# Attention and a ternary feed-forward net on one core: more blocks of P on their way, the looks at the weights in another order and without ScalarE, the flag made last

## The chip, the cores and the metric

The kernel runs on one core of a Trainium2 chip. The core has a matrix engine (TensorE, PE in the profile; its weight loads are PEld), three engines for elementwise work (VectorE or DVE, ScalarE or ACT, GpSimd or POOL) and SyncE (SP), which here only issues DMAs. The metric is device time in microseconds for one execution. Three runs of the kernel before gave 871.02, 871.73 and 874.87 us, median 871.73.

## The reference

```python
x: (2, 2048, 256)                                  # layer norm without weights, then
xn = layernorm(x)
q, k, v = xn @ Wq, xn @ Wk, xn @ Wv                # 256 x 256 each
attn = softmax(causal(q @ k.T) * 256 ** -0.5)
a = (attn @ v) @ Wo
h = silu(xn @ w1.T * s1) * (xn @ w2.T * s2)        # 1024 hidden, weights are -1, 0 or 1
h = gelu(h @ h1.T * s_h1); h = gelu(h @ h2.T * s_h2)
out = x + a + h @ w3.T * s3
```

All arrays are float32. The feed-forward weights are drawn from -1, 0 and 1, but the kernel may not take that for granted: it looks at them while it runs.

## The kernel before, in words

The program has two stages. The first is attention with everything beside it, to about 283 us in the profiled execution; the second is the feed-forward net, from there to the end. A flag, one number in memory, decides between two forms of the second stage: a fast one for weights that are whole and small (`ffn_ternary`), and a general one. All engines read the flag (L1175) and branch (L1176).

**Tiles.** The 2 x 2048 rows are eight blocks of 512 (n = 0 to 7, four to a batch), each of four tiles of 128 rows (t = 0 to 3). For one tile the keys come in blocks m of 512, up to n. `score(n, t, m)` is six products of 512 columns (L401: numbers are split in a high and a low part) into one of four PSUM banks; DVE copies the bank out and takes the row maximum (L410); after the last block ACT takes the exponentials (L422).

**Turning P.** The product of P with the values (`weigh`, L479 and L484: four products with 512 columns and four with 256 for a full block) needs P transposed. Small pieces are transposed by PE (L465). Most go another way, "by blocks": DVE transposes 32 x 32 squares (`turn_blocks`, L292), SP stores the result in DRAM (L297, d<-b), and SP fetches it back in another order, four DMAs to a unit of up to eight key tiles (`fetch_blocks`, L304, e<-d). Then `turn(n, t, m)` makes one block pT of it: ACT rounds the high part (L460), POOL subtracts for the low part (L461). There are two buffers for fetched units (pool `bp`, tile e) and four for pT (pool `ptp`, LEAD + 2 with LEAD = 2). `fetch_units` (L439) fetches the unit that is needed and, when a unit's first block is turned, one more.

**Order of work.** A planner written out by hand goes through the 32 tiles (loop at L721). In step j it scores tile j and weighs the tiles that are due: a tile by blocks is due 42000 columns of matrix work after its scores (DELAY_BLOCKS), others 9000. `weigh_steps` puts the turning of a block at most LEAD = 2 blocks ahead of the weighing (L518). `merged` interleaves both lists by their cost in columns. This gives the order in which the program is written; a scheduler with a model of the engines then fixes the order on each engine, and may move an instruction ahead of one that it holds to be waiting.

**The looks.** Beside this, `beside` (L642) spends every few thousand columns on one step of a list of looks at the weights, which are loaded by ACT's DMA queue into two buffers (stg, 128 x 1024). `low` is for w1, w2 and w3: POOL rounds w1 and w2 into their place for the second stage (L134, via L555), DVE masks the low bits (L558), ACT sums them (L560). `odd` is for h1 and h2: ACT takes absolute values (L565), DVE counts what is neither 0 nor 1 (L567); there are 16 such looks. For h1, DVE also forms four sums for the second stage (`sum_up`, L153), which SP stores. The order of the list is w1, w2, then in turns h1, h2 and w3 (L607 to L617). All these are put behind a marked instruction of the planner's on their engine (`tc.issue_after`). When no look is left, the flag is made: a maximum on DVE, a product of one number on PE (L744), a copy to memory on DVE (L745).

At the end PE makes the last quarter of a first product of the feed-forward net (L748 to L750, with L172), which is before the branch in PE's program.

**Second stage.** `ffn_ternary` multiplies by the seven-product scheme of Strassen and Winograd (L850); its first products are those of L172 with w1 and w2.

Of the kernel before, what the change touches and what calls it, by code (L numbers as in the profile page):

```python
# [9 lines left out]
F32 = mybir.dt.float32  # L10
F32R = mybir.dt.float32r
# [9 lines left out]
P = 128  # L21
TB = 512
# [10 lines left out]
LOOKS_FROM = 3  # L33
LEAD = 2
WARM = 14

# [3 lines left out]

SLOTS = {"h1": range(7), "h2": (0, 4, 1, 3, 2, 5, 6)}
LOW_BITS = 0xFFF

# [21 lines left out]
def attn_ffn_kernel(  # L65
# [123 lines left out]
    with ExitStack() as actx:  # L189
# [6 lines left out]
        sp = actx.enter_context(tc.tile_pool(name="sp", bufs=3))  # L196
        bp = actx.enter_context(tc.tile_pool(name="bp", bufs=2))
        ptp = actx.enter_context(tc.tile_pool(name="ptp", bufs=LEAD + 2))
        small = actx.enter_context(tc.tile_pool(name="small", bufs=4))
# [3 lines left out]
        xs, rstds, ks, qs, vs = {}, {}, {}, {}, {}  # L203
        turns = {"ps": 0, "b": 0, "q": 0}

# [4 lines left out]
        def bank():  # L210
            return in_turn("ps", ps_tiles)

        def load_x(n):
# [224 lines left out]

        def fetch_units(until, more):  # L439
            while units and (more or until not in fetched):  # L440
                more = more and until not in fetched
                n, t, u, k, d = units.pop(0)
                e = bp.tile([P, UK * P], F32, tag="e", name=f"e_{n}_{t}_{u}")[:, : k * P]
                fetched[n, t, u] = fetch_blocks(d, k, e)

        def turn(n, t, m):

            first = n - n % NB
            tiles = NT if m < n else t + 1
            w = tiles * P  # L450
            pT = ptp.tile([P, 2, TB], F32R, tag="pT", name=f"pT_{n}_{t}_{m}")
            state[n, t][m] = pT
            if by_blocks(n, t, m):
                u, at = divmod((m - first) * NT, UK)
                fetch_units((n, t, u * UK), at == 0)
                src = fetched[n, t, u * UK][:, ds(at, tiles)]
                hi, lo = (
                    pT[:, a, :w].rearrange("p (k i q) -> p k i q", k=tiles, q=Q) for a in range(2)
                )
                nc.scalar.copy(hi, src)  # L460
                nc.gpsimd.tensor_tensor(lo, src, hi.bitcast(F32), ALU.subtract)  # L461
                return
            pt = ps_t.tile([P, TB], F32, tag="pt", name=f"pt_{n}_{t}_{m}")
            for j in range(tiles):
                nc.tensor.transpose(  # L465
                    pt[:, ts(j, P)], state[n, t]["s"][:, ds((m - first) * TB + j * P, P)], ident
                )
            hi_lo(pT[:, 0, :w], pT[:, 1, :w], pt[:, :w])

        def weigh(n, t, m):  # L470
            first = n - n % NB
            st = state[n, t]
# [41 lines left out]
        def weigh_steps(g, until):  # L514

            steps = []
            while g < len(blocks) and blocks[g][0] <= until:
                while turned[0] <= min(g + LEAD, len(blocks) - 1) and (  # L518
                    turned[0] <= g or blocks[turned[0]][0] <= until + 1
                ):  # L520
                    b = blocks[turned[0]]
                    steps.append((0 if by_blocks(*b[1:]) else 2 * TB, lambda b=b: turn(*b[1:])))
                    turned[0] += 1
                _, n, t, m = blocks[g]
                steps.append((6 * TB if m < n else 6 * P * (t + 1), lambda b=blocks[g]: weigh(*b[1:])))
                g += 1
            return g, steps
# [34 lines left out]
        def odd(t):  # L562

            with tc.issue_after(marks["ACT"]):
                nc.scalar.activation(t, t, AF.Abs)  # L565
            with tc.issue_after(marks["DVE"]):
                nc.vector.scalar_tensor_tensor(  # L567
                    t, t, 0.0, t, ALU.not_equal, ALU.not_equal, accum_out=seen()
                )
# [36 lines left out]

        for src, dst in ((w1, w1_sb), (w2, w2_sb)):  # L607
            for c in range(src.shape[1]):
                item_low(src[:, c, :], dst[:, c, :])
        w3_at = list(range(0, HC, SC // D))  # L610
        for c in range(HK):
            item_factors(h1, factors["h1"], c)
            for k in (2 * c, 2 * c + 1):
                item_signs(h2[:, k, :])
# [104 lines left out]
        j = -1  # L719
        checked = False  # L720
        while until < len(tiles) - 1:  # L721
# [16 lines left out]
            merged(a, b, beside)  # L738
            if not looks and not checked:
                checked = True  # L740
                most = small.tile([P, 1], F32, tag="most", name="most")
                nc.vector.reduce_max(most, low_bits[:, : looked[0]], axis=AX.X)
                pf = bank()
                nc.tensor.matmul(out=pf[:1, :1], lhsT=most, rhs=ones, start=True, stop=True)  # L744
                nc.vector.tensor_copy(flag, pf[:1, :1])  # L745

        assert checked
        last_quarter = [bank(), bank()]  # L748
# [473 lines left out]
```

## Time and profile before

| | us |
|---|---|
| median of three runs | 871.73 |
| the profiled execution, its own time | 872.82 |
| its span, first to last instruction | 871.1 |
| PE busy in the span | 852.2 |
| DVE, ACT, POOL busy | 620.4, 504.9, 296.4 |
| start of the first L479, of the last quarter's L172, of the first L850 | 53.7, 283.6, 307.3 |

The profile is of one execution, taken by the hardware profiler. A row of the timeline has the start, the time that it covers, the engine, the line of the program, the operation, what it writes and reads, and in brackets the idle time ahead of it and who ended that. The windows give, for a stretch, the busy time of each engine and the share of full speed that was granted to PE's clock (PEclk). The end of a matrix product is modelled, and products overlap; the pace of PE is read from one start to the next.

### The profile page before, as it was taken

How to read it: one execution, taken by the hardware profiler on the slowest of the kernel's cores; microseconds unless marked ns; L12 is line 12 of the kernel's file. 1: busy time of each engine (PE TensorE's matmuls, PEld its weight loads, DVE VectorE, ACT ScalarE, POOL GpSimd, SP SyncE). 2: the span in 40 equal slices, each digit the busy share in tenths (PEclk: the TensorE clock that was granted, in tenths of full speed). 3: DMA queues.
4: the chain of work that ended last, by engine and by line, in shares of the span. 5: the costliest groups of instructions: out<-in, count | busy, mean ns of one | idle time of the engine just before them, and what ended most of it. 6: DMA issues, size and time to landing. Idle time of an engine off the chain costs nothing.

```text
span 871.1 us, 12205 instructions
## 1 busy us (share of the span) xinstructions
PE 852.2 (98%) x4280; PEld 720.1 (83%) x4280; DVE 620.4 (71%) x1065; ACT 504.9 (58%) x881; POOL 296.4 (34%) x242
## 2 busy tenths in 40 slices
PE   8999799999999999999999999999999999999997
PEld 5988688888887878888988888988888898888887
DVE  5687664784764699996596596569468648848764
ACT  2556556764666456677256586536557635657670
POOL 4034857433544476550142050025024003502300
PEclk8999989999999999999999999999999999999999
DMA  9876499766792898854334434432444431144411
GB/s 307 331 250 212 152 348 292 265 214 194 251 343 62 340 400 309 312 192 146 111 109 150 144 144 146 148 121 103 146 145 145 146 136 58 50 144 145 145 49 53
DMA packets 62679, 162.53 MB, mean 187 GB/s; under 512 B 6544, under 2 KB 36368, under 8 KB 53264
## 3 DMA queue, kind: packets, MB, share of 16 engines
q1 hardware_dynamic: 56048, 141.73, 46.6%
q10 hardware_dynamic: 5472, 15.73, 5.3%
q0 software_dynamic: 1088, 4.19, 1.2%
q8 instruction: 36, 0.59, 0.3%
q14 instruction: 35, 0.29, 0.1%
HBM read 120.21 MB, written 47.71 MB: 193 GB/s over the span
## 4 chain that ended last, share of the span: by engine, by line
PE 75%; DMA 9%; DVE 6%; issue 3%; ACT 3%; POOL 2%; SPq 2%; ACTq 0%; POOLq 0%; DVEq 0%
PE ps_own L850 23%; PE ps L850 23%; PE ps L172 5%; PE ps_own L172 5%; PE ps L401 5%; DMA e<-d 4%; PE ps_own L1011 4%; PE ps L1011 4%; POOL pT L461 2%; DMA d<-b 2%; PE ps L373 2%; PE po L479 2%; PE ps L357 2%; SPq L304 1%; DMA d_x<-b 1%
## 5 line engine op out<-in xcount | busy, mean ns | idle before, releaser
L401 PE MATMUL ps<-k,q 128*128 128x512 f32 (+3 forms) x480 | 109.6, 366 | 0.0
L461 POOL TENSOR_TENSOR pT<-e,pT 128x512 fp32r<-128x512 f32 (+3 forms) x60 | 74.8, 1264 | 72.5 <-ACT pT L460 55.6
L401 PEld LDWEIGHTS ps<-k,q 128*128 128x128 f32 x480 | 82.0, 189 | 12.2
L479 PE MATMUL po<-v,pT 128*128 128x512 f32 x272 | 79.6, 406 | 6.6 <-ACT pT L460 6.5
L982 POOL TENSOR_TENSOR rt<-rt,xt 128x1024 f32<-128x1024 f32 x8 | 21.5, 2706 | 165.2 <-issue 114.7
L871 ACT ACTIVATE k_h_u<-k_h_u,h_s_sb 128x512 f32<-128x512 f32 x64 | 45.9, 722 | 38.1 <-DVE k_h_u L870 37.5
L830 POOL TENSOR_TENSOR k_h_u<-k_h_p,k_h_u 128x512 f32<-128x512 f32 x16 | 23.2, 1452 | 123.1 <-ACT q L185 106.3
L479 PEld LDWEIGHTS po<-v,pT 128*128 128x128 f32 x272 | 48.1, 193 | 14.5 <-ACT pT L460 7.2
L410 DVE TENSOR_SCALAR_CACHE_REDUCE s<-ps 128x512 f32<-128x512 f32 (+3 forms) x80 | 47.1, 600 | 12.1 <-PE ps L407 8.1
L422 ACT ACTIVATE s<-s,low 128x1024 f32<-128x1024 f32 (+7 forms) x48 | 43.0, 898 | 21.7 <-DVE low L416 21.7
L292 DVE STREAM_TRANSPOSE b<-s 128x1024 f32<-128x1024 f32 (+3 forms) x30 | 33.5, 1128 | 22.8 <-ACT s L422 20.5
L460 ACT CAST pT<-e 128x512 fp32r<-128x512 f32 (+3 forms) x60 | 32.4, 574 | 27.4 <-DMA e<-d 25.0
L484 PEld LDWEIGHTS po<-v,pT 128*128 128x128 f32 x272 | 42.0, 190 | 6.5 <-POOL pT L461 1.7
L484 PE MATMUL po<-v,pT 128*128 128x256 f32 x272 | 46.9, 286 | 0.2 <-POOL pT L461 0.2
L186 DVE TENSOR_TENSOR q<-k_h_u,q 128x512 fp32r<-128x512 f32 x32 | 45.9, 1462 | 0.0
L889 POOL TENSOR_TENSOR k_h_p<-f_h_B,k_h_p 128x512 f32<-128x512 f32 x16 | 34.4, 2175 | 21.2 <-DVE h_h_T L186 21.2
L500 POOL TENSOR_TENSOR r<-r 128x256 f32<-128x256 f32 x32 | 24.4, 765 | 49.7 <-ACT r L499 49.7
L830 POOL TENSOR_TENSOR f_w_B<-f_w_B,f_w_B 128x512 f32<-128x512 f32 x16 | 26.0, 1646 | 33.0 <-DVE f_w_B L181 33.0
L172 PE MATMUL ps<-xh,w_sb 128*128 128x512 f32 x144 | 35.9, 392 | 0.0
L870 DVE TENSOR_TENSOR k_h_u<-ps_own,k_h_u 128x512 f32<-128x512 f32 x32 | 21.7, 686 | 17.8 <-PE ps_own L850 17.8
L871 ACT ACTIVATE k_h_p<-k_h_p,h_s_sb 128x512 f32<-128x512 f32 x32 | 22.8, 722 | 18.6 <-DVE k_h_p L870 18.6
L850 PE MATMUL ps<-q,w_h_A 128*128 128x512 f32 x128 | 31.2, 393 | 1.5 <-DVE f_w_B L181 1.5
(176 smaller groups left out, 2201.3 us busy)
## 6 DMA issues: line engine op xcount, KB each, us to landing
w_h_S<-factors_h SPq DMA_DIRECT2D x32, 1024.0 KB, 4.7
w_h_A<-factors_h SPq DMA_DIRECT2D x24, 1024.0 KB, 4.7
d<-b SPq DMA_DIRECT2D x18, 512.0 KB, 3.5
e<-d SPq DMA_DIRECT2D x72, 128.0 KB, 3.6
xT_d<-k SPq DMA_DIRECT2D x8, 1024.0 KB, 7.3
stg<-in_ffn_h_w ACTq DMA_DIRECT2D x16, 512.0 KB, 5.6
x<-in_attn_x SPq DMA_DIRECT2D x16, 256.0 KB, 5.9
factors_h<-xh SPq DMA_DIRECT2D x4, 1024.0 KB, 4.8
```

The costliest lines, as they stand in the source:

```text
L172: nc.tensor.matmul(out=p, lhsT=w[:, c, ts(o, P)], rhs=xh[:, c, a, :], start=(c == 0 and a == 0), stop=(c == DC - 1 and a == 1),)
L186: nc.vector.tensor_tensor(r[:, 1, :], f, r[:, 0, :].bitcast(F32), ALU.subtract)
L401: nc.tensor.matmul(out=ps[:, :w], lhsT=qs[n][:, c, a, ts(t, P)], rhs=ks[m][:, c, b, :w], start=(k == 0), stop=(m < n and k == 3 * DC - 1),)
L410: marks["DVE"] = nc.vector.tensor_scalar(st["s"][:, ds(at, w)], ps[:, :w], 1.0, None, ALU.mult, ALU.max, accum_out=st["tops"][:, m - first ...
L422: marks["ACT"] = nc.scalar.activation(st["s"][:, at], st["s"][:, at], AF.Exp, bias=low, accum_out=st["sums"][:, u // UK : u // UK + 1],).ins
L461: nc.gpsimd.tensor_tensor(lo, src, hi.bitcast(F32), ALU.subtract)
L479: nc.tensor.matmul(out=st["po"], lhsT=pT[:, 0, ts(j, P)], rhs=vs[m][:, j, :, :], start=(m == first and j == 0), stop=False,)
L484: marks["PE"] = nc.tensor.matmul(out=st["po"][:, 0, :], lhsT=pT[:, 1, ts(j, P)], rhs=vs[m][:, j, 0, :], start=False, stop=(m == n and j == ...
L830: nc.gpsimd.tensor_tensor(B["B12"][i], B["B22"][i], B["B12"][i], ALU.subtract)
L850: nc.tensor.matmul(out=out[o], lhsT=w[:, c, ts(o, P)], rhs=sets[right][c][:, a, :], start=(start and c == 0 and a == 0), stop=(c == HK - 1 ...
L871: nc.scalar.activation(C[k][o], r[o] if r else banks[o], AF.Gelu, scale=s[:, at : at + 1])
L1011: nc.tensor.matmul(out=ys[t][:, :D], lhsT=h[c][:, a, ts(t, P)], rhs=w3_sb[:, c, :], start=(c == 0 and a == 0), stop=(c == HC - 1 and a == 1),)
```

## The change

It does seven things.

1. Fetched units rotate over four memories instead of two, and blocks pT over six instead of four. The new memory is that of w1 (two more for units) and w2 (two more for blocks), which hold nothing until the looks at w1 and w2 put it there. From tile (6, 0) on (`WIDE`), units go to the four buffers of x and the blocks use the two own unit buffers in place of w2's.
2. `fetch_units` fetches whenever fewer than four units are fetched and not yet turned to the end.
3. A block that is turned by blocks may be turned four blocks ahead of the weighing (LEAD_BLOCKS = 4); one that PE transposes stays at two.
4. The looks at w1 and w2 move from the head of the list to behind h1's last item.
5. `odd` takes the absolute value on DVE, by masking the sign bit, and not on ACT.
6. The flag is made just ahead of the last weighing, its product behind the marked product on PE.
7. The pool `bp` goes.

```diff
+LEAD_BLOCKS = 4
+MAGNITUDE = 0x7FFFFFFF
-        bp = actx.enter_context(tc.tile_pool(name="bp", bufs=2))
-        ptp = actx.enter_context(tc.tile_pool(name="ptp", bufs=LEAD + 2))
+        ptp = actx.enter_context(tc.tile_pool(name="ptp", bufs=1))
...
+        pT_tiles = [ptp.tile([P, 2, TB], F32R, name=f"pT_{i}") for i in range(4)]
+        e_tiles = [ptp.tile([P, UK * P], F32R, name=f"e_{i}") for i in range(2)]
+        w_memory = [
+            [w.rearrange("p c h -> p (c h)")[:, ts(i, UK * P)] for i in range(2)] for w in (w1_sb, w2_sb)
+        ]
+        WIDE = (N - 2, 0)
+        def pT_tile(n, t):
+            more = e_tiles if (n, t) >= WIDE else w_memory[1]
+            tile = in_turn("pT", pT_tiles + more)
+            return tile if len(tile.shape) == 3 else tile.rearrange("p (a t) -> p a t", a=2)
+        def e_tile(n, t):
+            if (n, t) >= WIDE:
+                return xp.tile([P, NT, D], F32, tag="x", name=f"e_{n}_{t}").rearrange("p t d -> p (t d)")
+            return in_turn("e", e_tiles + w_memory[0]).bitcast(F32)
...
-        def fetch_units(until, more):
-            while units and (more or until not in fetched):
-                more = more and until not in fetched
+        def fetch_units():
+            while units and len(fetched) < 4:
                 n, t, u, k, d = units.pop(0)
-                e = bp.tile([P, UK * P], F32, tag="e", name=f"e_{n}_{t}_{u}")[:, : k * P]
-                fetched[n, t, u] = fetch_blocks(d, k, e)
+                fetched[n, t, u] = fetch_blocks(d, k, e_tile(n, t)[:, : k * P])
...
                 src = fetched[n, t, u * UK][:, ds(at, tiles)]
+                if at + tiles == fetched[n, t, u * UK].shape[1]:
+                    del fetched[n, t, u * UK]
...
+        def judge():
+            most = small.tile([P, 1], F32, tag="most", name="most")
+            nc.vector.reduce_max(most, low_bits[:, : looked[0]], axis=AX.X)
+            with tc.issue_after(marks["PE"]):
+                pf = bank()
+                nc.tensor.matmul(out=pf[:1, :1], lhsT=most, rhs=ones, start=True, stop=True)
+            nc.vector.tensor_copy(flag, pf[:1, :1])
         def weigh(n, t, m):
+            if (n, t, m) == (N - 1, NT - 1, N - 1):
+                judge()
...
-                while turned[0] <= min(g + LEAD, len(blocks) - 1) and (
-                    turned[0] <= g or blocks[turned[0]][0] <= until + 1
-                ):
+                while turned[0] < len(blocks):
                     b = blocks[turned[0]]
+                    lead = LEAD_BLOCKS if by_blocks(*b[1:]) else LEAD
+                    if turned[0] > g and (turned[0] > g + lead or b[0] > until + 1):
+                        break
...
         def odd(t):
-            with tc.issue_after(marks["ACT"]):
-                nc.scalar.activation(t, t, AF.Abs)
             with tc.issue_after(marks["DVE"]):
+                nc.vector.tensor_scalar(t.bitcast(U32), t.bitcast(U32), MAGNITUDE, None, ALU.bitwise_and)
                 nc.vector.scalar_tensor_tensor(
                     t, t, 0.0, t, ALU.not_equal, ALU.not_equal, accum_out=seen()
                 )
...
-        for src, dst in ((w1, w1_sb), (w2, w2_sb)):
-            for c in range(src.shape[1]):
-                item_low(src[:, c, :], dst[:, c, :])
         for c in range(HK):
             item_factors(h1, factors["h1"], c)
+            if c == HK - 1:
+                for src, dst in ((w1, w1_sb), (w2, w2_sb)):
+                    for i in range(DC):
+                        item_low(src[:, i, :], dst[:, i, :])
```

The old place of the flag, behind `merged` in the planner's loop (L739 to L745), is removed.

More of the change, by code (lines that the diff above doesn't have):

```diff
@@ L203, in attn_ffn_kernel @@
         xs, rstds, ks, qs, vs = {}, {}, {}, {}, {}
-        turns = {"ps": 0, "b": 0, "q": 0}
+        turns = {"ps": 0, "b": 0, "q": 0, "pT": 0, "e": 0}
         def in_turn(key, tiles):
@@ L211, in bank @@
             return in_turn("ps", ps_tiles)
+        pT_tiles = [ptp.tile([P, 2, TB], F32R, name=f"pT_{i}") for i in range(4)]
[3 more added lines that the diff above has]
+        ]
+        assert DC * H == 2 * UK * P and UK * P == 2 * TB == NT * D
+        WIDE = (N - 2, 0)
[7 more added lines that the diff above has]
+            return in_turn("e", e_tiles + w_memory[0]).bitcast(F32)
         def load_x(n):
@@ L450, in turn @@
             w = tiles * P
-            pT = ptp.tile([P, 2, TB], F32R, tag="pT", name=f"pT_{n}_{t}_{m}")
+            pT = pT_tile(n, t)
             state[n, t][m] = pT
@@ L454, in turn @@
                 u, at = divmod((m - first) * NT, UK)
-                fetch_units((n, t, u * UK), at == 0)
+                fetch_units()
                 src = fetched[n, t, u * UK][:, ds(at, tiles)]
+                if at + tiles == fetched[n, t, u * UK].shape[1]:
+                    del fetched[n, t, u * UK]
                 hi, lo = (
@@ L468, in turn @@
             hi_lo(pT[:, 0, :w], pT[:, 1, :w], pt[:, :w])
+        def judge():
+            assert not looks
+            most = small.tile([P, 1], F32, tag="most", name="most")
[4 more added lines that the diff above has]
+            nc.vector.tensor_copy(flag, pf[:1, :1])
         def weigh(n, t, m):
+            if (n, t, m) == (N - 1, NT - 1, N - 1):
+                judge()
             first = n - n % NB
@@ L719, in attn_ffn_kernel @@
         j = -1
-        checked = False
         while until < len(tiles) - 1:
@@ L738, in attn_ffn_kernel @@
             merged(a, b, beside)
[L739 to L747, printed above, removed]
         last_quarter = [bank(), bank()]
```

## The prediction

> **What bounds the kernel now.** I read the page's busy rows first, then what PE waited for, then the windows around the largest wait, then PE and ACT there in order of time.
>
> ```profile
> PE 852.2 (98%) x4280; PEld 720.1 (83%) x4280; DVE 620.4 (71%) x1065; ACT 504.9 (58%) x881; POOL 296.4 (34%) x242
> ...
> PEclk8999989999999999999999999999999999999999
> ```
>
> PE is busy in 852.2 of 871.1 us, so nothing can be won but PE's idle time and the time in which its clock is low. One slice of attention, the sixth (109 to 131 us), shows a low clock. What PE waited for, with total, times and longest:
>
> ```profile
> PE po L479 <- ACT pT L460: 6.5, 4, 4.8
> ...
> PE ps L357 <- DVE v L252: 0.5, 1, 0.5
> ...
> PE ps L357 <- DVE s L410: 0.3, 1, 0.3
> ...
> PE po L484 <- POOL pT L461: 0.2, 1, 0.2
> ```
>
> These four are in attention after the start (first L479 at 53.7): 7.5 us, of which 6.7 are waits for a block pT, and one alone is 4.75. PE in order of time around it:
>
> ```profile
> 99.55 1.08 PE L479 MATMUL po<-v,pT 128*128 128x512 f32 x4
> 100.46 0.64 PE L484 MATMUL po<-v,pT 128*128 128x256 f32 x4
> 100.94 1.09 PE L479 MATMUL po<-v,pT 128*128 128x512 f32 x4
> ...
> 108.89 2.08 PE L479 MATMUL po<-v,pT 128*128 128x512 f32 x4 [4.75 <-ACT pT L460]
> 110.78 1.22 PE L484 MATMUL po<-v,pT 128*128 128x256 f32 x4
> 111.80 1.81 PE L479 MATMUL po<-v,pT 128*128 128x512 f32 x4
> 113.45 0.86 PE L357 MATMUL ps<-k,wqk 128*128 128x512 f32 x3
> ```
>
> After the gap the same three groups take longer from start to start: 1.89, 1.02 and 1.65 us, against 0.93 (100.94 to the next group at 101.87), 0.48 (100.46 to 100.94) and 0.93 without it. That is 0.96 + 0.54 + 0.72 = 2.2 us more, and the windows 100 to 110 and 110 to 120 both have a PEclk of 0.83. So the gap costs 4.75 + 2.2 = **7.0 us**. Why ACT was late, and behind whom:
>
> ```profile
> 103.29 0.19 ACT L422 ACTIVATION_READ_ACCUMULATOR s<-s,low 128x1 f32 x1
> 107.28 1.06 ACT L565 ACTIVATE stg<-stg 128x1024 f32<-128x1024 f32 x1 [3.80 <-DVE xh L153]
> 108.24 0.60 ACT L460 CAST pT<-e 128x512 fp32r<-128x512 f32 x1
> ```
>
> ```profile
> 102.14 4.38 DVE L153 TENSOR_TENSOR xh<-stg,stg 128x512 fp32r<-128x512 f32 x1
> 106.55 0.69 DVE L153 TENSOR_TENSOR xh<-xh,stg 128x512 fp32r<-128x512 f32 x1
> ```
>
> ACT stood at the absolute value of a look (L565), which waited for DVE's sums of the same buffer; L460 was next in its queue. One sum took 4.38 us where the next took 0.69, while POOL ran L500, L461 and two L339 without a break (102.37 to 105.96). The unit itself was there sooner: its four fetches were issued from 99.56 to 100.86, and e<-d lands in 3.6 us in the median, so by about 104.5.
>
> **Part 5, looks without ScalarE.** It removes 16 x 1.05 us (L565) from ACT, and with them the only look there that waits for DVE's sums; nothing of it was on PE's path but the gap above. Alone it would bring L460 to about 104.5, and the gap from 4.75 to about 0.9 (104.5 plus 0.5 for the rounding, against 104.1), too short a gap for the low clock by the other gaps of this trace (0.9 at 274, clock 1.00). Gain 3.9 + 2.2 = 6.1.
>
> DVE gets 16 masks. The nearest row is L558, also a mask on 128 x 1024 words: 0.69 to 1.76 us, median 1.07. So 11 to 28 us more for DVE, I take 17.1. From 50 to 275 us DVE is busy 153.8 of 225 (68%); it becomes 76%. It lies beside PE unless DVE falls behind by more than the four PSUM banks cover; the cost is bounded below by 0 and above by another gap like this one, 7.0. What DVE costs PE now (L252 and L410, 0.5 + 0.3) is the nearest row; I take **1.0 more**.
>
> The Trainium skill, page "SBUF — State Buffer", section "SBUF: two separate sides", speaks against this part: DVE and POOL share a port pair that one of them holds for a whole instruction, if DVE's has two inputs from SBUF or runs in a two-port mode, while ACT has its own ports. By that rule each mask could stand behind a subtraction of POOL's (L461, mean 1264 ns), some 20 us more of DVE as an estimate. The trace agrees with the rule for the 4.38 us sum, and for masks only mildly: one of six L558 is at 1.76.
>
> **Parts 1 to 3, more on their way.** By the planner's columns (512 in about 0.22 us: four L479 in 0.93), around the gap, for tiles (3, 0) and (2, 3), a unit is now fetched 4608 to 9216 columns before its first block is turned, 2 to 4 us, no more than a landing. With the change I count 25344 to 36864, 11 to 16 us. From turning to weighing it goes from 4608 to 9216 columns (2 to 4 us) to 10752 to 14080 (4.7 to 6 us). The remaining waits for pT (6.5 - 4.75 + 0.2 = 2.0 us) are of this kind: the one at 274.19 (0.91) follows a fetch that was issued at 269.65, and tile (7, 2)'s second unit moves from 8704 columns ahead to 33536. I count **2.0** as gone, and the 0.9 that part 5 leaves. Bounds: 0 and 2.9. No DMA is added: 72 fetches, each 0.43 us on SP's queue, only earlier. They now stand 2304 to 41472 columns behind the unit's scores. The ten or so below 10000 (4 us) wait on SP for their own store to land, and behind them wait the next store (d<-b) and the store of sums; they have 13 us and more until they are turned, so this costs nothing unless a hold outlasts that. One tile (5, 0) is turned 13824 columns after its scores, as before.
>
> **Part 4, w1 and w2 late.** The same instructions, moved. The four roundings (L134, 1.08) and masks go from 65 to 93 us to about 205 to 230. They must come after tile (5, 3)'s blocks are read (turned 16000 columns, 7 us, before the first) and before the first quarter (46000 columns, 20 us, after the last). Behind a rounding that waits stands POOL's next L461, four blocks ahead of its need. The sums of h1 come earlier instead, at about 62 us, where DVE is fullest:
>
> ```profile
> 50.00:75.00 25.00, 25.00 (x130) 21.39 (x129) 22.21 (x70) 14.17 (x28) 10.94 (x10) 1.00 0.57 192
> ```
>
> (columns: PE, PEld, DVE, ACT and POOL busy, PEclk, DMA share, GB/s). DVE has 22.21 there; minus two masks (1.8), plus four sums (2.8), plus two looks at 1.07 + 1.23 + 0.08 (4.8) is 28.0 in 25. DVE ends 3.0 us late, 6.7 if one sum takes 4.38 again. PE writes a bank again after four groups of six products, each 1.4: 5.6 us without weighing between, 11 with. So up to 1.1; it is inside the 1.0 above. The next window (14.38) takes the backlog.
>
> **Part 6, late flag.** Now the flag is made at 273.19 and PE reads it at 282.02. Then its product stands between 282.2 and 282.4, with 0.14 for the copy (DVE is idle from 281.5 to 285.8), 0.49 for the read and 0.09 for the branch: done at about 283.5, while PE has products until 285.5 (eight of the last quarter at 0.23 from 283.64). Free by 2 us; **0**. If the step to the copy takes as long as now (271.04 to 273.19, DVE busy) it is done at 285.3, still in time; upper bound 0.5, none below 0.
>
> **Sum.** 4.75 + 2.2 + 2.0 - 1.0 = 8.0 us less. The profiled execution's own 872.82 (1.7 over its span) becomes 864.8; it stood 1.1 above the median, so against the median of 871.73 I predict **863.7**. The second stage, from the first L850 at 307.3 to the end 563.8 us, stays.
>
> **Rivals.** (a) *The gap comes back elsewhere.* The order on each engine is fixed from a model that does not know the 4.38; DVE and POOL still block each other, and a sum in its new place holds L252 or L410, so a bank, or SP's store of sums (L581 was issued at 108.00, the next fetch behind it at 108.48). For it: 16 sums stay, DVE is fuller. Against: one of 16 did it, and pT has twice the lead. One gap of the present kind: -9.0 + 7.0 = -2.0, 869.7.
>
> (b) *The lead does not come about.* A fetch waits for its store, and the order on the engines is by readiness, so blocks are not turned sooner; then part 5 alone acts: -6.1 + 1.0 = -5.1, 866.6. For it: the two DMAs take 3.5 + 3.6 us whatever the buffers. Against: turned at the earliest 10.7 us after the scores (but for one tile, which is then weighed 21 us later), a unit has landed.
>
> (c) *Slower: DVE becomes what PE waits for.* The first item's four sums and four looks now lie at about 62 to 91 us, beside the row statistics and transposes that fill DVE there. If three of the four sums take 4.38 and not 0.69, DVE is 3.0 + 3 x 3.7 = 14 us late, more than the 11 that the banks cover. PE then stops, starts and stops again when the next item does the same, each time with the low clock after it: 2 x 7.0 - 9.0 = +5.0, 876.7. It decides from a backlog of 11 us. For it: 28.0 in 25. Against: 76% on average, and POOL loses the four roundings in that window.
>
> The Trainium skill, page "TensorE: Matmul & The Clock Gate", section "What's actually happening", has PE's clock halved after an idle window of about 3.4 us. By it a stop of 2 us would cost 2 and not 4; the trace shows the low clock only after the 4.75.
>
> **Chances.** Forecast 0.50, (b) 0.16, (a) 0.22, (c) 0.12. About 0.5% (4.4 us) is what a measurement of this kernel can tell from no change: faster than 867.4 are the forecast and (b), 0.65 with a little lost at the edge; the same 0.23; slower 0.12. Range: at the low end all 7.5 + 2.2 are gone and the one gap at the head of the second stage (1.23, at 314.10) too: 871.7 - 10.9 = 860.8, with the runs' own spread (0.7) 860.2. At the high end (a) with 1.8 for DVE: 871.5. It leaves out (c).
>
> **What would show it.** Right: no wait of L479 for L460 over 1 us, PEclk 1.00 in all windows from 25 to 283, the last quarter at about 275, DVE 11 to 28 us busier, and 563.8 us from the first L850 to the end. Wrong: a wait of PE for L252, L410 or a bank over 2 us, a second slice with a low clock, PE idle after the flag's product, or new waits in the second stage.

## The result and the profile after

The changed kernel takes 880.43 us (median of 7 runs, 878.10 to 881.61), the kernel before in the same session 872.74 (7 runs): the ratio is 1.0095, with a 95% interval of 1.0075 to 1.0115. It is **slower**, by 0.95%, where 0.9% faster was forecast. The profiled execution has a span of 878.7 us against 871.1.

From the page after, the rows that answer to those of before:

```profile
PE 853.8 (97%) x4280; PEld 721.3 (82%) x4280; DVE 642.7 (73%) x1081; ACT 489.0 (56%) x865; POOL 302.4 (34%) x242
...
PEclk9999989999999999999999999999999999999999
```

PE's work is the same; DVE has 22.3 us more (forecast 17.1, bounds 11 to 28), ACT 15.9 less. One slice has a low clock, the sixth again. What PE waited for, after:

```profile
PE po L518 <- DVE pT L273: 3.9, 1, 3.9
PE po L513 <- ACT pT L272: 2.7, 3, 1.4
PE po L513 <- ACT pT L482: 2.0, 1, 2.0
PE ps L422 <- DVE v L273: 1.6, 2, 1.3
PE ps L174 <- ACT b L182: 1.4, 1, 1.4
```

(L513 and L518 are the products of L479 and L484 before, L482 the rounding of L460, L272 and L273 the two halves of an eviction that were L251 and L252.) The wait for blocks turned by blocks went from 6.5 us to 2.0. In its place PE waits for blocks that PE itself transposes (L272, L273: 6.6 us), which are still turned at most two ahead, and for v, b and banks. In all, PE idles 13.6 us between 25 us and the second stage's first product, against 7.6.

**Where the 8.5 us come from.** The first Strassen product (L876, before L850) starts at 315.8, not at 307.3; from there to the end it is 562.9 (before 563.8). So all is lost in the first stage. Up to 60 us nothing is: PE idles 0.9 us more in the first 25 us, but its clock is slow there for 3.4 us and not for 6.8, and its three-hundredth product starts at 60.2 where it started at 60.3. Behind that, 6.0 us are the idle time just named, and some 1.7 come from a further stretch of slow clock (3.4 us at half speed), which follows the wait of 2.02 us at 228.29. About 0.8 is in no wait that the profile shows. The windows of after:

```profile
110.00:120.00 10.00, 5.47 (x17) 4.42 (x18) 10.00 (x14) 3.38 (x8) 4.58 (x6) 0.67 0.43 149
...
230.00:240.00 10.00, 10.00 (x51) 8.65 (x50) 6.32 (x17) 5.59 (x12) 5.42 (x5) 0.86 0.79 240
```

In 110 to 120 DVE is busy for 10.00 of 10 us and PE for 5.47. What DVE did there, and then POOL beside it:

```profile
107.93 7.04 DVE L155 TENSOR_TENSOR xh<-stg,stg 128x512 fp32r<-128x512 f32 x1
114.89 0.55 DVE L273 TENSOR_TENSOR pT<-pt,pT 128x384 fp32r<-128x384 f32 x1
...
115.42 0.67 DVE L155 TENSOR_TENSOR xh<-xh,stg 128x512 fp32r<-128x512 f32 x1
```

```profile
105.58 2.54 POOL L483 TENSOR_TENSOR pT<-e,pT 128x512 fp32r<-128x512 f32 x2
108.09 2.52 POOL L483 TENSOR_TENSOR w_sb<-w_sb 128x512 fp32r<-128x512 f32 x2
110.57 0.73 POOL L534 TENSOR_TENSOR r<-r 128x256 f32<-128x256 f32 x1
111.27 2.46 POOL L360 TENSOR_TENSOR k<-x,k 128x512 fp32r<-128x512 f32 x2
113.70 0.71 POOL L534 TENSOR_TENSOR r<-r 128x256 f32<-128x256 f32 x1
```

One sum of DVE's (L155, before L153) takes 7.04 us; the next takes 0.67. It began while POOL was in a string of two-input instructions, ran through six more of them, and ended at 114.97, 0.56 after the string broke (113.70 + 0.71). Behind it on DVE stood L273, the low part of the very next block, and PE stood behind that:

```profile
115.49 1.01 PE L518 MATMUL po<-v,pT 128*128 128x256 f32 x3 [3.94 <-DVE pT L273]
116.29 1.91 PE L513 MATMUL po<-v,w_sb 128*128 128x512 f32 x4
```

So the one large gap of before (4.75 at 108.89, behind a sum of 4.38) has come back at 115.49 behind a sum of 7.04, with the same slow clock after it (1.71 us from 116.29 to the next group at 118.00, where 0.93 is the pace at full speed). It costs about what it cost before: 3.94 and some 2.3 by the clock, against 4.75 and 2.2. So it is a gain that did not come; the 8.5 us are the stops beside it.

**Not all of these stops are DVE's.** Two of them come from blocks on their way through DRAM. PE, ACT and SP at each, in order of time:

```profile
94.67 0.60 PE L487 MATMUL pt<-ident,s 128*128 128x128 f32 x4
98.53 1.14 ACT L482 CAST pT<-e 128x512 fp32r<-128x512 f32 x2 [5.30 <-DMA e<-d]
99.58 0.58 ACT L272 CAST pT<-pt 128x512 fp32r<-128x512 f32 x1
100.21 1.19 PE L513 MATMUL po<-v,pT 128*128 128x512 f32 x4 [1.40 <-ACT pT L272]
...
218.79 1.75 SPq L325 DMA_DIRECT2D e<-d  x4
227.62 1.14 ACT L482 CAST pT<-e 128x512 fp32r<-128x512 f32 x2 [4.63 <-DMA e<-d]
228.29 0.98 PE L513 MATMUL po<-v,pT 128*128 128x512 f32 x3 [2.02 <-ACT pT L482]
```

At 98.53 ACT had stood 5.30 us at fetched blocks that were not there yet. The block that PE needed next, transposed by PE itself from 94.67 on, stood behind them in ACT's queue (L272), and PE lost 1.40 us. At 228.29 PE needed the fetched block itself. SP issued that unit's four fetches from 218.79 on, as its store had just landed (218.77, issued at 213.43); they landed from 226.65 to 227.56, 7.5 to 7.9 us after their issue, where the median before is 3.6. Two loads of w1 and w2, which part 4 moved there, and one of 1 MB (xh) were under way at the same time; whether they made the fetches slow is not shown. With the slow clock after it this stop costs 3.7 us, and both together 5.1 of the 8.5.

**The theories.** P: DVE's sums stand behind strings of POOL's two-input instructions, and PE behind DVE; the change let the strings grow. A: a longer lead costs, since ACT rounds a block that isn't there yet and holds up its queue. D: sixteen more masks are too much for DVE. F: the late flag. O: any new order of the program costs some tenths of a per cent, because the order of before is a lucky one.

### The profile page after: what moved, and what is told of

The parts are those of the page before. It is cut to its first block, busy times and chain, and to the rows that moved or that the text cites. A ratio compares the mean times of both kernels' runs of the same rounds, so it can differ in the third digit from the quotient of the medians.

```text
span 878.7 us, 12208 instructions
## 1 busy us (share of the span) xinstructions
PE 853.8 (97%) x4280; PEld 721.3 (82%) x4280; DVE 642.7 (73%) x1081; ACT 489.0 (56%) x865; POOL 302.4 (34%) x242
## 4 chain that ended last, share of the span: by engine, by line
PE 74%; DMA 10%; DVE 7%; issue 3%; SPq 2%; ACT 2%; POOL 1%; POOLq 0%; ACTq 0%; DVEq 0%
PE ps_own L876 23%; PE ps L876 22%; PE ps L174 6%; PE ps_own L174 5%; PE ps L422 4%; DMA e<-d 4%; PE ps_own L1037 3%; PE ps L1037 3%; DMA d<-b 2%; PE po L513 2%; SPq L325 2%; PE ps L394 2%; DMA d_x<-b 1%; PE ps L378 1%; DMA stg<-in_ffn_w_w 1%
## 5 line engine op out<-in xcount | busy, mean ns | idle before, releaser
L422 PE MATMUL ps<-k,q 128*128 128x512 f32 (+3 forms) x480 | 111.6, 370 | 1.6 <-DVE v L273 1.6
L513 PE MATMUL po<-v,pT 128*128 128x512 f32 x182 | 53.8, 401 | 4.8 <-ACT pT L272 2.7
L431 DVE TENSOR_SCALAR_CACHE_REDUCE s<-ps 128x512 f32<-128x512 f32 (+3 forms) x80 | 47.2, 598 | 6.0 <-PE ps L428 2.8
L483 POOL TENSOR_TENSOR pT<-e,pT 128x512 fp32r<-128x512 f32 (+2 forms) x24 | 29.5, 1246 | 53.2 <-ACT pT L482 53.1
L513 PEld LDWEIGHTS po<-v,pT 128*128 128x128 f32 x182 | 31.6, 189 | 10.5 <-ACT pT L272 3.2
L534 POOL TENSOR_TENSOR r<-r 128x256 f32<-128x256 f32 x32 | 29.2, 913 | 30.9 <-ACT r L533 30.9
L518 PEld LDWEIGHTS po<-v,pT 128*128 128x128 f32 x182 | 28.7, 190 | 8.5 <-DVE pT L273 4.8
L518 PE MATMUL po<-v,pT 128*128 128x256 f32 x182 | 31.7, 286 | 3.9 <-DVE pT L273 3.9
L174 PEld LDWEIGHTS ps<-xh,w_sb 128*128 128x128 f32 x144 | 26.5, 188 | 8.2 <-ACT b L182 1.8
L876 PE MATMUL ps<-q,w_h_A 128*128 128x512 f32 x128 | 31.2, 393 | 1.5 <-DVE f_w_B L183 1.3
```

What stands on the lines that cost most here:

```text
L174: nc.tensor.matmul(out=p, lhsT=w[:, c, ts(o, P)], rhs=xh[:, c, a, :], start=(c == 0 and a == 0), stop=(c == DC - 1 and a == 1),)
L422: nc.tensor.matmul(out=ps[:, :w], lhsT=qs[n][:, c, a, ts(t, P)], rhs=ks[m][:, c, b, :w], start=(k == 0), stop=(m < n and k == 3 * DC - 1),)
L431: marks["DVE"] = nc.vector.tensor_scalar(st["s"][:, ds(at, w)], ps[:, :w], 1.0, None, ALU.mult, ALU.max, accum_out=st["tops"][:, m - first ...
L513: nc.tensor.matmul(out=st["po"], lhsT=pT[:, 0, ts(j, P)], rhs=vs[m][:, j, :, :], start=(m == first and j == 0), stop=False,)
L518: marks["PE"] = nc.tensor.matmul(out=st["po"][:, 0, :], lhsT=pT[:, 1, ts(j, P)], rhs=vs[m][:, j, 0, :], start=False, stop=(m == n and j == ...
L876: nc.tensor.matmul(out=out[o], lhsT=w[:, c, ts(o, P)], rhs=sets[right][c][:, a, :], start=(start and c == 0 and a == 0), stop=(c == HK - 1 ...
```

## The experiments

Ratios are to the kernel before, in the same session, whose median was between 871.05 and 872.74 us.

### One part alone: odd_on_dve and w_last

odd_on_dve is the kernel before with part 5 alone, w_last with part 4 alone.

```diff
# odd_on_dve
-            with tc.issue_after(marks["ACT"]):
-                nc.scalar.activation(t, t, AF.Abs)
             with tc.issue_after(marks["DVE"]):
+                nc.vector.tensor_scalar(t.bitcast(U32), t.bitcast(U32), MAGNITUDE, None, ALU.bitwise_and)
# w_last
-        for src, dst in ((w1, w1_sb), (w2, w2_sb)):
-            for c in range(src.shape[1]):
-                item_low(src[:, c, :], dst[:, c, :])
...
+            if c == HK - 1:
+                for src, dst in ((w1, w1_sb), (w2, w2_sb)):
+                    for i in range(DC):
+                        item_low(src[:, i, :], dst[:, i, :])
```

> The kernel before with part 5 alone: the absolute values on DVE. Theory P (POOL's unbroken strings hold DVE's two-input sums; the lead makes the strings longer): without the lead the strings are as before, ACT no longer stands behind the sums, and the 4.75 us gap with its slow clock goes; 864 to 868 us. Theory A (rounding four blocks ahead makes ACT wait for fetches): the same, since the lead is not changed; 864 to 868. Theory D (16 masks more are too much for DVE): 876 to 880, with PE waiting for L252 or L410.

> The kernel before with part 4 alone: w1 and w2 looked at last. Theory P: the second item's sums fall where POOL also scales and subtracts for the turned keys; a sum of 4 us or more and a gap of PE behind it, 872 to 880. Theory A: order of looks does not matter, 870 to 875. Theory D: no mask is added, 870 to 875.

odd_on_dve: 874.35 us, 1.0039 (1.0024 to 1.0055). This part was to gain 6.1 - 1.0, and no theory's range holds the time: P and A had 864 to 868, D 876 to 880. Its trace shows why the gain does not come. POOL, then DVE, then PE:

```profile
99.77 1.31 POOL L462 TENSOR_TENSOR pT<-e,pT 128x512 fp32r<-128x512 f32 x1
101.04 0.74 POOL L501 TENSOR_TENSOR r<-r 128x256 f32<-128x256 f32 x1
101.74 0.46 POOL L462 TENSOR_TENSOR pT<-e,pT 128x128 fp32r<-128x128 f32 x1
102.15 2.52 POOL L340 TENSOR_TENSOR k<-x,k 128x512 fp32r<-128x512 f32 x2
104.63 2.49 POOL L462 TENSOR_TENSOR pT<-e,pT 128x512 fp32r<-128x512 f32 x2
```

```profile
100.46 7.21 DVE L154 TENSOR_TENSOR xh<-stg,stg 128x512 fp32r<-128x512 f32 x1
...
109.04 1.29 DVE L566 TENSOR_SCALAR stg<-stg 128x1024 uint32<-128x1024 uint32 x2
...
113.67 0.68 DVE L411 TENSOR_SCALAR_CACHE_REDUCE s<-ps 128x512 f32<-128x512 f32 x1
```

```profile
106.52 1.09 PE L480 MATMUL po<-v,pT 128*128 128x512 f32 x4
114.41 2.08 PE L358 MATMUL ps<-k,wqk 128*128 128x512 f32 x4 [6.79 <-DVE s L411]
```

The same stretch of POOL before:

```profile
101.11 1.30 POOL L461 TENSOR_TENSOR pT<-e,pT 128x512 fp32r<-128x512 f32 x1
...
103.49 2.47 POOL L339 TENSOR_TENSOR k<-x,k 128x512 fp32r<-128x512 f32 x2
108.92 1.81 POOL L461 TENSOR_TENSOR pT<-e,pT 128x512 fp32r<-128x512 f32 x1 [2.95 <-ACT pT L460]
```

Before, POOL had the same string up to the two L339, and then nothing to do until 108.92, since ACT stood at the absolute value and made no new pT. That pause let the sum in after 4.38 us. Now ACT goes on, POOL gets two more subtractions (104.63, 2.49 us), the string is 2.5 us longer and the sum 2.8. PE's wait is no longer for pT but for a bank that DVE has to clear (L411): 6.79 us. Between the held sum's end at 107.67 and L411 DVE works off 6 us more: two sums, two counts, a transpose, and the two masks that this part added (1.2 of the 6). **In this trace ACT's wait was not only a cost: it was what broke POOL's string.**

w_last: 878.09 us, 1.0076 (1.0054 to 1.0098). A part that I priced at nothing loses 6.6 us by itself (0.0076 of 872). P had asked for a sum of 4 us or more; no sum is long in its trace (1.65 at most). It has four stops of middling length instead, the last of them ahead of the last quarter, and three stretches of slow clock (with the first, the second and the last):

```profile
PE po L479 <- ACT pT L460: 3.3, 1, 3.3
PE ps L401 <- DVE v L252: 2.5, 1, 2.5
PE po L484 <- DVE pT L252: 2.0, 1, 2.0
PE ps L172 <- ACT b L180: 1.6, 1, 1.6
```

### Both parts together, and the rest: parts_4_5, after_lead2, after_flag_old, after_abs_act

parts_4_5 is the kernel before with both edits above. The other three are the changed kernel with one thing undone.

```diff
# after_lead2
-LEAD_BLOCKS = 4
+LEAD_BLOCKS = 2
# after_abs_act
+            with tc.issue_after(marks["ACT"]):
+                nc.scalar.activation(t, t, AF.Abs)
...
-                nc.vector.tensor_scalar(t.bitcast(U32), t.bitcast(U32), MAGNITUDE, None, ALU.bitwise_and)
# after_flag_old: in the planner's loop, not ahead of the last weighing
+            if not looks and not checked:
+                checked = True
+                judge()
```

In after_flag_old the flag's product also loses its place behind the marked one.

> The kernel before with parts 4 and 5 together, without the blocks, units, lead and flag. If parts 1 to 3 gain nothing: as the changed kernel, 877 to 881, with a sum of DVE of 6 us or more at 100 to 115 us. If the lead does its work in the changed kernel: 882 to 886 here, with waits for pT in sum above those of the changed kernel. If the lead is what costs: 872 to 876.

> The changed kernel with LEAD_BLOCKS = 2; four units are still fetched. Theory A: ACT's waits for fetches fall from 54 us to under 20, as blocks are rounded later and units are there sooner; 868 to 873. Theory P: strings on POOL become shorter, the longest sum falls from 7.0 to 4 us or less; 868 to 876. Theory D: DVE has as many masks, 878 to 882.

> The changed kernel with the flag made where it was, when no look is left. If the late flag costs at the branch: 1 to 2 us less than the changed kernel (878 to 879). If not, as PE shows no wait there: 879 to 881, and the gaps of 0.71 and 1.42 us ahead of the last quarter stay.

> The changed kernel with part 5 undone: absolute values on ACT again. Theory D: DVE is relieved, 870 to 874, gaps behind L273 and L431 gone. Theory P: the 7.04 us sum and a gap of 4 us or more stay, and ACT stands behind sums as well; 878 to 886. Theory A: ACT's head waits for fetches stay at about 50 us; 878 to 884.

| kernel | us | ratio (interval) | longest sum | largest stop of PE |
|---|---|---|---|---|
| parts_4_5 | 879.12 | 1.0085 (1.0072 to 1.0098) | 5.52 | 3.96 |
| after_lead2 | 881.61 | 1.0123 (1.0100 to 1.0146) | 7.07 | 4.40 |
| after_flag_old | 879.33 | 1.0093 (1.0068 to 1.0118) | 6.58 | 4.04 |
| after_abs_act | 879.47 | 1.0102 (1.0082 to 1.0123) | 6.63 | 3.16 |

Parts 4 and 5 alone are as slow as the whole change (1.0085 against 1.0095, intervals overlapping): parts 1 to 3, the extra memory and the lead, bring nothing and cost nothing that can be measured. In parts_4_5 the largest stop (at 248.80) stands behind POOL's L462, not behind a sum. Theory A falls as far as the lead is concerned: with a lead of two it is no faster. So does P's reading that the lead lengthens the strings, as a sum of 7.07 us is there with a lead of two. F falls: the flag's place makes no difference that can be measured, and in after PE waits nowhere for it. Undoing part 5 alone heals nothing either (after_abs_act, where D had 870 to 874): there, too, a sum is held for 6.63 us, so the string grows without part 5's help once the order is new.

What did change is how long ACT stands at fetched blocks. What ACT waited for, first before, then after:

```profile
ACT pT L460 <- DMA e<-d: 25.0, 11, 5.3
```

```profile
ACT pT L482 <- DMA e<-d: 29.7, 8, 7.0
...
ACT e L482 <- DMA e<-d: 11.7, 3, 5.3
...
ACT w_sb L482 <- DMA e<-d: 5.7, 2, 4.8
```

25.0 us became 47.1 (29.7 + 11.7 + 5.7; e and w_sb are the new places of blocks pT). That is not the lead's: with a lead of two it is 47.2, where A had asked for under 20. Parts 4 and 5 alone, without new memory or lead, have 41.7; the changed kernel with the absolute values back on ACT has 27.8. It fits that ACT, with less to do, comes to the fetches sooner. Not all of this is harmless, as the stops at 100.21 and 228.29 show. But after_abs_act, with almost as little of it as the kernel before, is no faster than the change, so it is not the whole loss.

### The sums taken off DVE: before_sums_act, after_sums_act, w_last_sums_act

h1's sums are left out; ACT copies one operand into each one's place, so h1's factors are not the reference's.

```diff
-            with tc.issue_after(marks["DVE"]):
-                sums_of_factors(sums, tiles, (i,), nc.vector)
+            (a11, a21), (a12, a22) = ((t[:, :HB], t[:, HB:]) for t in tiles)
+            with tc.issue_after(marks["ACT"]):
+                nc.scalar.copy(sums[:, i, :], (a21, a11, a12, a11)[i])
```

> The kernel before with the sums left out in the same way (copies on ACT; h1's factors are not the reference's). Theory P: the 4.75 us gap and its slow clock go, 7 us; 863 to 867. Theory O: only the place of the gap changes; 869 to 875.

> The changed kernel with the sums left out: in place of each sum of two quarters ACT copies one quarter (so h1's factors are not the reference's). DVE then has no instruction of the looks with two different inputs from memory but the counts. Theory P (a two-input instruction of DVE stands until POOL's string breaks, 7.0 us): the gap of 3.94 us with its slow clock goes, 6 us; 872 to 876, the rest being part 4's gaps. Theory O (the order of looks by itself, whatever DVE does): a gap of 3 us or more stays between 100 and 120 us; 877 to 882.

> Part 4 alone and the sums left out (copies on ACT; h1's factors are not the reference's). It stands against part 4 alone (878.1) and the kernel before with the sums left out (868.2). Theory P: part 4 costs through the sums, 867 to 870. Theory O: part 4 costs through its late looks (gaps at 160, 247 and ahead of the last quarter, 6 us in all), 873 to 876.

| | with sums on DVE | without (interval) | sums cost |
|---|---|---|---|
| before | 1 | 0.9962 (0.9946 to 0.9978) | 0.4% |
| part 4 alone | 1.0076 | 0.9974 (0.9961 to 0.9987) | 1.0% |
| the change | 1.0095 | 1.0010 (0.9992 to 1.0028) | 0.85% |

(868.16, 869.73 and 872.16 us.) This speaks for theory P: with sixteen sums of some 0.7 us each on DVE the changed kernel takes about 7.4 us more (0.85%, a difference of two ratios, as all in the last column), and without them part 4 costs 0.1% (0.9974 against 0.9962, intervals overlapping) and not 0.8. So part 4's loss goes with the sums too, though none of them was long in its trace. How they cost there is not shown: PE's largest stop in w_last, 3.3 us, stands behind two absolute values on ACT (2.00 us). Nor does the trace of the change put 7.4 us behind a sum, only 3.94 and the slow clock after it. Each of these kernels is also a new order, which by itself moved the time by 0.3 to 0.5% in the controls below; 0.85 and 1.0 lie beyond that, 0.4 does not. For before_sums_act P had 863 to 867. Its 868.16 is 3.3 us less by the ratio, half of what the gap (7.0) was held to cost. In the change without sums, a mask of part 5 (L600) is held instead: 4.53 us at 109.41, through four instructions of POOL's. What is left over the kernel before without sums is 0.5%.

### The sums on GpSimd, and its strings cut: sums_pool, after_sums_pool, keys_later, after_keys_later, sums_pool_keys_later

sums_pool lets POOL make the sums, behind its last subtraction for a block. keys_later puts the scaling of the keys (L339, L340, two instructions in the string) behind that mark too.

```diff
-                nc.gpsimd.tensor_tensor(lo, src, hi.bitcast(F32), ALU.subtract)
+                marks["POOL"] = nc.gpsimd.tensor_tensor(lo, src, hi.bitcast(F32), ALU.subtract).ins
# sums_pool
-            with tc.issue_after(marks["DVE"]):
-                sums_of_factors(sums, tiles, (i,), nc.vector)
+            with tc.issue_after(marks["POOL"]):
+                sums_of_factors(sums, tiles, (i,), nc.gpsimd)
# keys_later
-            xn = start_keys(n).rearrange("p t d -> p (t d)")
+            with tc.issue_after(marks["POOL"]):
+                xn = start_keys(n).rearrange("p t d -> p (t d)")
```

In after_sums_pool the first sums, which come before any such subtraction, stand behind DVE's mark.

> The kernel before with the sums made on POOL, behind the last turned block, so DVE has no sum that can be held; the result is the reference's. Theory P: the gap of 4.75 us goes, but POOL gets 16 instructions of 1.3 us among the blocks, 21 us; 866 to 872. Theory O: 872 to 878.

> The changed kernel, with h1's sums made by GpSimd, behind its last subtraction for a turned block, instead of by DVE. Theory P (DVE's sums stand behind GpSimd and PE behind DVE; that is what the change made worse): the stop of 3.9 us and the slow clock after it go, as with the sums left out (1.001 of before), so 0.998 to 1.004; most of the loss is gone. Theory L (more blocks on their way are worth something once the sums do no harm): the new kernel comes down to or under the kernel before with the same sums on GpSimd (0.9951). If it stays above that, parts 1 to 3 give nothing that can be measured. Theory O (any new order costs half a per cent, whatever the sums): about 1.004 to 1.01, as now.

> The kernel before with the scaling of the turned keys on POOL put behind the last turned block, so that all 16 do not run at 88 to 103 us. Theory P: POOL has breaks, the longest sum falls from 4.38 to under 2 us, and the gap with its slow clock goes: 863 to 867. If the string of blocks alone holds DVE: a sum of 3 us or more stays, 869 to 873.

> The changed kernel with the scaling of the turned keys put behind the last turned block on POOL. Theory P (the crowd on POOL at 88 to 115 us holds DVE): the 7.04 us sum shortens to under 3 us and the 3.94 us gap with its slow clock goes; 872 to 875. If the string of blocks alone does it: 878 to 882.

> The kernel before with both: sums on POOL and the keys' scaling spread. Theory P: as sums left out (868) or better, 864 to 869. Theory O: any new order, 870 to 877.

| kernel | us | ratio (interval) |
|---|---|---|
| sums_pool | 866.68 | **0.9951** (0.9933 to 0.9969) |
| after_sums_pool | 874.54 | 1.0036 (1.0015 to 1.0058) |
| keys_later | 872.10 | 1.0003 (0.9984 to 1.0022) |
| after_keys_later | 874.26 | 1.0031 (1.0015 to 1.0048) |
| sums_pool_keys_later | 869.64 | 0.9985 (0.9966 to 1.0004) |

In the kernel before, keys_later does what P asked for: the longest sum falls from 4.38 to 1.78 us, and the gap and its slow clock are gone. But the time stays, where P had 863 to 867: PE idles 7.2 us in the first stage behind 25 us, against 7.6, in other places (the longest stop 2.62). So the long sum alone did not set the time. In the changed kernel, cutting POOL's strings (no sum over 1.6 us) takes 0.64% of its 0.95% away. **sums_pool beats both kernels**, by 0.5% and 1.4%. From its page and its waits of PE:

```profile
PE 850.4 (98%) x4280; PEld 719.4 (83%) x4280; DVE 610.1 (71%) x1049; ACT 504.7 (58%) x881; POOL 318.0 (37%) x258
```

```profile
PE po L479 <- ACT pT L460: 3.0, 4, 1.7
PE ps L357 <- DVE s L410: 1.3, 1, 1.3
```

Sixteen instructions and 10.3 us went from DVE, 21.6 us came to POOL, and PE's longest wait for a block is 1.7 us (before: 4.8). Both edits together gain less than the first alone.

after_sums_pool should have come under 0.9951 if more blocks on their way were worth something; it is 0.85% above. Here DVE's masks and counts of part 5 are held in the sums' place; DVE, then POOL:

```profile
100.67 5.27 DVE L601 SCALAR_TENSOR_TENSOR stg<-stg 128x1024 f32<-128x1024 f32 x1
```

```profile
99.85 2.54 POOL L483 TENSOR_TENSOR pT<-e,pT 128x512 fp32r<-128x512 f32 x2
102.34 2.52 POOL L360 TENSOR_TENSOR k<-x,k 128x512 fp32r<-128x512 f32 x2
107.13 0.74 POOL L534 TENSOR_TENSOR r<-r 128x256 f32<-128x256 f32 x1 [2.27 <-ACT r L533]
```

The count ran through three of POOL's instructions and ended 1.1 us after the last of them (104.86), its own length. A mask that began at 157.85 took 5.9.

### Other orders: signs_first, nudge

```diff
# signs_first: in the list of looks, h2's item ahead of h1's
-            item_factors(h1, factors["h1"], c)
...
+            item_factors(h1, factors["h1"], c)
# nudge: the looks begin one step later
-LOOKS_FROM = 3
+LOOKS_FROM = 4
```

> The kernel before with one change in the order of looks: in each turn the two signs of h2 come before h1's item, so that the first sums do not meet the scaling and turning of the second batch's keys on POOL at 88 to 106 us. Theory P: no sum above 3 us, the gap goes; 863 to 868. Theory O: any new order brings gaps of its own, in sum as large as now; 870 to 878.

> A control: the kernel before, the looks begun one tile later (LOOKS_FROM = 4), nothing else. Theory O: any new order on the engines brings other gaps; 872 to 880, and gaps that were not there before. Theory P alone: the first sums come later, past the keys' scaling, so 864 to 869.

signs_first: 874.40, 1.0034 (1.0016 to 1.0053). nudge: 875.98, 1.0045 (1.0032 to 1.0058). Nothing was added or taken away in either. In signs_first no sum takes over 1.77 us, as P asked (863 to 868), and yet it is slower. In nudge one sum takes 3.41 us, and PE's waits are spread: 5.0 us for L460 in five, 2.7 for L410, 2.6 for b ahead of the last quarter. So O holds in part: two new orders without other work cost 0.34 and 0.45%, and of the 0.95% about half may be no more than that.

### The two engines by themselves: port, port_late

Two small kernels without the reference's work: POOL runs a string of subtractions of 128x512, DVE does one instruction beside it. port varies the string's length and DVE's operation, port_late the moment at which DVE's instruction comes.

```python
# port_late: DVE copies 0 to 896 columns from PSUM to PSUM, then comes the subtraction
for n in range(6):
    nc.gpsimd.tensor_tensor(pT[n][:, 1, :], e[:, ts(n, TB)], e[:, ts((n + 1) % 6, TB)], ALU.subtract)
...
nc.vector.tensor_tensor(v, c, d, ALU.subtract)
```

> Not the reference's computation (the output is zeros): a measurement by itself. POOL runs a string of 1, 2, 4 or 8 instructions of 128 x 512 without a break, and DVE, released at the string's head, runs two instructions of 128 x 512. Theory P: a DVE subtraction with two inputs from memory takes the rest of the string (about 1.2, 2.5, 5 and 10 us) and its second 0.69; alone it takes 0.69; one with an input from a bank takes 0.69 beside any string. Theory S (both share the path): DVE's takes about twice 0.69 beside any string.

> A small kernel that computes nothing of the reference (its output is zeros): strings of six subtractions of 128x512 on GpSimd, and DVE's subtraction of 128x512 with two inputs in SBUF, which becomes ready after 0 to 896 columns of copying from PSUM to PSUM, so that it arrives early or late in one of GpSimd's instructions (1.26 us alone). Theory H (an instruction of DVE that arrives late in GpSimd's is passed over until the string ends): some arrivals take 3 to 7 us and end about 0.6 us after the last of the six. Theory S (it only waits for the end of the one that runs, as in the small kernel before): all take 0.7 to 1.9 us, wherever they arrive, and the long ones of the large kernel need something that this one lacks.

port: DVE's subtraction takes 0.68 us alone and 1.66 to 1.68 beside a string of 1, 2, 4 or 8; POOL's next instruction then takes 1.71 and not 1.26. A mask takes 0.42 alone, 1.39 to 1.41 beside a string. With one input in PSUM it is 0.68 both ways. port_late, at three arrivals, DVE and then the string beside the first:

```profile
15.90 1.46 DVE L96 TENSOR_TENSOR v<-c,d 128x512 fp32r<-128x512 f32 x1
...
50.67 0.72 DVE L96 TENSOR_TENSOR v<-c,d 128x512 fp32r<-128x512 f32 x1
...
68.05 1.68 DVE L96 TENSOR_TENSOR v<-c,d 128x512 fp32r<-128x512 f32 x1
```

```profile
15.55 7.81 POOL L83 TENSOR_TENSOR pT<-e 128x512 fp32r<-128x512 f32 x6
```

All sixteen take 0.68 to 1.68 us: the rest of the one instruction that POOL is in, plus about 0.55. Theory S of the two: a late arrival alone does not make DVE wait for the whole string.

The Trainium skill, page "SBUF — State Buffer", section "SBUF: two separate sides", says just this, that the loser is blocked for the other's whole instruction. The small kernels agree (1.66 us); the 7.04 us and 7.21 us of the large ones go beyond it.

Over the eighteen traces of the large kernels 330 of DVE's sums, masks and counts begin inside a two-input instruction of POOL's. 318 end before a further one has passed, and one lets one pass. 11 let two to six pass and take 3.41 to 7.21 us, all but one between 99 and 110 us; each of these ends 0.55 us (a count 1.1) after POOL's string does. **What makes these eleven different stays open.** It is not the length of the string (1 to 8 alike in port), nor the moment of arrival (0.12 to 1.02 us were left of POOL's instruction, and others that came with as little left were served at once). The small kernels have no PE, ACT or DMA traffic beside the string; that was not tried.

## Why the prediction was wrong

**The gap (4.75 + 2.2 less): failed.** The step was: with L565 off ACT, L460 runs at 104.5 and the gap shrinks to 0.9. The rounding did come early (at 102.56 in odd_on_dve). But the step took the 4.38 us of the sum as given, and ACT's wait behind it as the only way to PE. odd_on_dve shows that ACT's wait set the 4.38: without it the sum took 7.21, and PE's wait went to the bank (6.79). The lines were there: POOL idled from 105.96, the sum ended at 106.5, and I named both without asking what POOL would do if ACT went on. The size was too large as well: no kernel won the 7.0 of the gap when it went. before_sums_act won 3.3 us by its ratio, sums_pool 4.3, keys_later nothing.

**DVE fuller (1.0 more): mis-sized.** Part 5 alone costs 3.4 us net (0.0039 of 872), where 5.1 were to be gained. The busy time was right (22.3 us for 11 to 28; the masks by themselves 18.0 for 17.1); 76% on average says nothing about a stop of 7 us. The rule that I weighed against the part, of the port that DVE and POOL share, pointed the right way, and I let one mask of six speak against it.

**Part 4 (nothing): mis-sized.** Alone it costs 6.6 us by its ratio, 0.1% without the sums. nudge lost 0.45% by its order alone, so part of it may be that. I looked at the places where w1 and w2 go and at how full DVE gets, and not at what else moves when everything behind them on four engines moves.

**Other waits for pT (2.0 less): failed.** Without the one large gap 2.0 us of such waits were left, and 2.0 us are there after. parts_4_5 has 9.0 us of waits for turned blocks, the change 2.0 and after_lead2 2.7, so parts 1 and 2 may have kept them down; the lead of four is not needed for it. But waits for blocks of PE's own turning, with the lead they always had, rose from none to 6.6. And the one wait of 2.02 us speaks against the step that a unit has landed when its turn comes. I reckoned with 3.5 us for its store and 3.6 for its fetches; here they took 5.3 and 8.8 (213.43 to 227.56), and ACT stood at the unit from 223.0 on. With the clock that cost 3.7 us.

**Right:** the flag costs nothing that can be measured (after_flag_old), the second stage stays (562.9 against 563.8). Of the rivals, (a) named what happened (the gap back elsewhere, sums blocked by POOL, L252 or a bank late) but let the other waits go with it and gave 869.7; (c) had the sign and, in part, the cause, at 876.7 with two large stops, where there was one and many small ones, some of them behind ACT and the fetches. I gave (c) 0.12, since it asked for a backlog of 11 us at 62 to 91 us. None came there: one sum of 7 us, just ahead of the one instruction that PE needed, made a gap like the old one. (The low end of the range, 871.7 - 10.9 - 0.7, is 860.1 and not 860.2; nothing hangs on it.)

Not shown: how much of the 0.95% is the sums' strings, how much ACT's waits for fetches and how much any new order's. They overlap, as the order decides which sum meets which string; nudge (0.45%) and the change without sums (0.10%, or 0.5% over the kernel before without them) are the bounds that the runs give.

## What to carry to other kernels

Before a wait is taken away, ask what it holds back: here ACT's wait was the pause in which DVE got its turn beside POOL. Moving the sums, which made DVE and POOL contend, to POOL gained 0.5% in the kernel before (sums_pool, 0.9951) and 0.6% in the changed one; that is little more than an order alone can move the time. In a program at 98% of its bound with the order fixed by a planner, an edit that moves many instructions should be priced with a control that only shifts the order, here some 0.4% slower. And a gap's length is not what its removal brings: with the long sum and its gap gone, keys_later took as long as before, since other waits came in its place.

## What the runs showed of the hardware

DVE's instruction with its inputs in SBUF waits for the one of POOL's that runs, 1.66 us for 0.68 (port), but was passed by up to six in the large kernels (7.21 us). With one input in PSUM it did not wait (0.68).

A slow clock does not need a long stop. I had said that it follows only the 4.75 of that trace. In sums_pool it follows one of 1.66 us; the window in which that wait ends, with PEclk in the third place from the right:

```profile
140.00:150.00 10.00, 9.68 (x47) 8.40 (x48) 2.99 (x12) 5.73 (x14) 8.20 (x8) 0.83 0.77 222
```

The wait ends at 140.32, and the clock is at half from 141.4 to 144.8. In keys_later a stop of 2.62 us is followed by no slow clock. What decides between them the runs do not show, but the slow stretches of all these traces, up to the second stage, last 3.4 us or twice that (6.8).

The Trainium skill, page "TensorE: Matmul & The Clock Gate", section "What's actually happening", has a free-running window of about 3.4 us in which activity is judged. The lengths agree with it; that a stop of 1.66 us can bring the slow clock and one of 2.62 need not is more than I took from it.
